# Layer 2 of a four-layer graph network on one core: diffusions moved into the end of the step before, blocks of layer 3 into the end of the second step

## The chip, the cores and the metric

The kernel runs on one core of one Trainium2 chip. Its engines are TensorE (PE in the profile, with PEld for its weight loads), VectorE (DVE), ScalarE (ACT), GpSimd (POOL) and SyncE (SP, which here only issues DMAs). The metric is the device time of one execution in microseconds. Each engine works through its own instructions in order, and waits in front of one whose data or buffer is not ready.

## What is computed

Four graph layers over 4096 nodes with 256 features, each followed by a residual and a layer norm. The change concerns layer 2 and the start of layer 3:

```python
def L2(X, S, W1, W2, W3, U1, U2, ln_g, ln_b):
    R = S + eye(N);  R = R / R.sum(-1, keepdims=True)
    Z = 0;  Xf = X;  Xa = X
    for n in range(2):
        A = top_p_attention(Xa, W1, W2, W3)
        Xf = R @ Xf
        Xa = A @ Xa
        Z = Z + Xf @ U1[n].T + Xa @ U2[n].T
    h = X + Z
    return layernorm(h) * ln_g + ln_b

def L3(x, adj, W, b):
    agg = adj @ x / maximum(adj.sum(1), 1)
    return relu(concat([x, agg]) @ W + b)

x = layernorm(x + L2(x, adj, ...))
x = layernorm(x + L3(x, adj, ...))
```

`top_p_attention` is a softmax over all nodes, of which each row keeps its largest entries up to a sum of 0.9, renormalised.

## The kernel before, in words

The 4096 rows are 32 blocks of 128 (`NB = 32`, b is a block). Layer 2 runs two steps. In both, the matrix that the adjacency multiplies lies in `XD`: for each block 512 columns, a rounded part and its remainder. A **diffusion** of block b is 32 matmuls of 512 columns into one PSUM bank, fed by eight pieces of the adjacency (256 KB each, four matmuls each, `adj_piece`, three buffers in turn, L176 and L179). Layer 3's product has the same shape; `early` (L1490 to L1498) is the same work for layer 3's first blocks, with the identity subtracted on POOL (L1493) from the piece that holds the block's own rows.

One **pass** of a step's loop handles block b in eight parts `s`: PE gathers the attention rows of block b (`gather`, L1300, from transposes `turn`, L1291), computes the scores of block b+2 (L935), and does the diffusion of block b+2, spread over the parts by the list `pieces`. DVE meanwhile selects the top entries of block b+1 (`nucleus`, L1072 to L1144: a threshold, two passes over the row, the largest 40, the edges, and eight multiplications in place at L1143). ACT exponentiates, copies transposes out of PSUM and estimates the next threshold (`guessed`). POOL adds up rows and, in step 1, normalises. Step 1's passes also close block b-1 (`closing`, the norms of layer 2) and, two blocks back, multiply the result by layer 3's weights (`turned`, `weighted`, `ahead3`, L1384, L1393, L1466 to L1468).

The order of the instructions in the loops is written by hand for PE, ACT, DVE and POOL (`manual_schedule`). Elsewhere, and for SP everywhere, a planner with a cost model orders them; it may also put later instructions into gaps of a hand-ordered stretch.

Around the steps stand:

- **Step 0's end.** The last pass (b = 30) has no diffusion and no scores left. DVE finishes block 31 and computes a verdict over all blocks (`settled`, L1187 to L1212), for which PE transposes twice (L1204, L1208). The verdict goes to DRAM, every engine reads it and branches past a repair (`mend`, L1157). Then block 31 is gathered, interleaved with step 1's `keys` (L848 to L899).
- **Between the steps.** The step's result rows are reloaded into `XD`, 1 MB for four blocks (`reload`, L1151).
- **Step 1's beginning.** Scores and threshold of block 0, `spreads` (L908 to L926), then sixteen projections of two blocks (`project`: PE at L1419, ACT copies at L1432 and L1434, a DMA in at L1431, an addition on POOL at L1435, a DMA out issued by ACT at L1436). The scores of block 1 stand in the middle of the projections. Then the diffusions of blocks 0 and 1, and the loop.
- **Step 1's end.** In the last pass blocks 0 and 1 of layer 3 are begun (seven pieces each). Then block 31 is gathered and closed, the repair is branched past, and behind it stand block 2 of layer 3 and, from weights in `kT` that DVE casts (`cast3`, L1703), block 3. All of them wait for the last row of `XD`, written from block 31's result (L1468). Layer 3 then does one block after another (L1738), with its weights cast by DVE and ACT (L1703, L1705) and its closing on DVE and ACT.

Of the kernel before, what the change touches and what calls it, by code (L numbers as in the profile page):

```python
# [9 lines left out]
F32 = mybir.dt.float32  # L10
# [45 lines left out]
class Net:  # L56
# [686 lines left out]
    def layer2(self):  # L743
# [3 lines left out]
        with ExitStack() as ctx:  # L747
# [312 lines left out]
            def nucleus(step, b, c, low, far, thr, pm=None, gw=None, sq=None):  # L1060
# [80 lines left out]
                for j in range(T):  # L1141
                    ec = e[:, j * 512:(j + 1) * 512]
                    nc.vector.scalar_tensor_tensor(ec, ec, edge[:, j:j + 1], ec, op0=ALU.is_ge, op1=ALU.mult)  # L1143
                nc.vector.reciprocal(r, r)  # L1144
# [8 lines left out]
            def mend(step, row, flag, e, r, h=None, pairs=None):  # L1153
# [3 lines left out]
                with tc.If(flag == 0):  # L1157
# [16 lines left out]
                    if step == 1:  # L1174
                        reload(xtd, 0, NB - 4)
                        for k in range(2):
                            nc.tensor.matmul(pairs[:, k], kT[:, :P], XD[:, 0].rearrange("p s d -> p (s d)"),
                                             start=False, stop=True)
                        whole(both(pairs))

            def settled():
# [24 lines left out]
                nc.vector.tensor_reduce(each, pt[:NB, :P], AX.X, ALU.min)  # L1206
                pt = psum.tile([P, 512], F32, name="ps_tp")
# [192 lines left out]
            def project(step, b):  # L1400
# [29 lines left out]
                else:  # L1430
                    nc.sync.dma_start(xb, rows(xd[two, :, 0, :]))  # L1431
                    nc.scalar.copy(X[:, two, :], pl[:, :, :D])  # L1432
                    xs = work.tile([P, 2, D], F32, name="part", bufs=1)
                    nc.scalar.copy(xs, pl[:, :, D:])  # L1434
                    nc.gpsimd.tensor_add(xb, xb, xs)  # L1435
                    nc.scalar.dma_start(rows(xd[two, :, 0, :]), xb)  # L1436
# [47 lines left out]
            def early(ps, b, groups):  # L1484

                for g in groups:
                    a = work.tile([P, 4, P], F32R, name="adj_piece", bufs=3)
                    nc.sync.dma_start(a.bitcast(F32), self.adjs[b, :, 4 * g:4 * g + 4, :])  # L1490
                    k = b - 4 * g
                    if 0 <= k < 4:
                        nc.gpsimd.tensor_sub(a[:, k, :], a[:, k, :].bitcast(F32), self.ident)  # L1493
                    for k in range(4):
                        jc = 4 * g + k
                        if jc == NB - 1:
                            yield a
                        nc.tensor.matmul(ps, a[:, k, :], XD[:, jc].rearrange("p s d -> p (s d)"),  # L1498
                                         start=(jc == 4), stop=(jc == NB - 1))
                    yield  # L1500

            def both(pairs):

                for b in range(2):
                    yield from early(pairs[:, b], b, (1, 2, 3, 4, 5, 6, 0))

            weights(0)
            for step in range(2):
# [7 lines left out]
                rs, edge = {}, nucleus(step, 0, *guess)  # L1516

                for b in range(0, NB, 2):
                    if b == 16:
                        whole(scores(1, queries(1)))  # L1520
                        guess = drained(guessed(step, 1))
# [11 lines left out]
                xb = base(step, 0)  # L1533
                pr = whole(diffusion(step, 0))
                whole(diffused(step, 0, pr, xb))
                whole(keep(step, 0, xb))
                pr = whole(diffusion(step, 1))
                aTs = [turn(es[0], g) for g in range(2)]
                q, xb = queries(2), base(step, 1)
                xc, pa, done, guessing = None, None, {}, iter(())  # L1540
                pieces = (0, 0, 2, 1, 2, 1, 2, 0) if step == 0 else (0, 0, 2, 1, 1, 2, 1, 1)
                with tc.manual_schedule(engines={ET.PE, ET.Activation, ET.DVE, ET.Pool}):
                    for b in range(NB - 1):
                        ahead = b + 2 < NB
                        edge = nucleus(step, b + 1, *guess)
                        if ahead:
                            score = scores(b + 2, q)
                            beside = diffusion(step, b + 2)
                        close, kept, put = None, None, None
                        if step == 1 and not ahead:  # L1550
                            pairs = psum.tile([P, 2, 512], F32, name="ps_logit", bufs=2)
                            beside = both(pairs)
                            nas = [t[:, i * 2048:(i + 1) * 2048].bitcast(U8).rearrange("p (k i) -> p k i", k=8)
                                   for t in (es[2], es[0]) for i in range(2)]
                            self.load_bytes(nas[:2], 0, 0)
                            pieces = (0, 2, 2, 2, 2, 2, 2, 2)
                        for s in range(8):
                            if s == 0:
# [6 lines left out]
                                difs = diffused(step, b + 1, pr, xb)  # L1565
                                next(difs)
                                kept = keep(step, b + 1, xb)
# [13 lines left out]
                            if ahead or step == 1:  # L1581
                                for _ in range(pieces[s]):
                                    next(beside)
# [8 lines left out]
                            if s in (2, 4, 6):  # L1592
# [5 lines left out]
                            if s == 6:  # L1598
                                if ahead:
                                    xb = base(step, b + 2)  # L1600
# [12 lines left out]
                            if s == 0:  # L1613
# [8 lines left out]
                        if not ahead:  # L1622
                            row = result(row)
                            if step == 1:
# [194 lines left out]
```

## Time and profile before

Three runs took 4100.99, 4105.11 and 4111.95 us, the median is 4105.11. The profiled execution took 4103.01 us; its span, from the first to the last instruction, is 4101.3. All times below are microseconds from the start of the span.

| engine | busy us | share of the span | instructions |
|---|---|---|---|
| PE | 3911.0 | 95% | 25081 |
| PEld | 3380.8 | 82% | 25081 |
| DVE | 3002.8 | 73% | 6655 |
| ACT | 2757.6 | 67% | 5127 |
| POOL | 1062.5 | 26% | 1300 |

| group | count | busy us | mean ns |
|---|---|---|---|
| gather, L1300 | 4096 | 971.9 | 380 |
| diffusion, L179 | 2048 | 579.2 | 418 |
| transposes, L1291 | 2048 | 308.2 | 273 |
| scores, L935 | 1024 | 275.3 | 410 |

Matmuls overlap in the array, so a group's time is less than count times mean: 32 products of layer 3 (L1738) end 7.47 us after each other. Step 0's loop runs from about 1812 to 2654, step 1's from about 2854 to 3767; layer 3's steady products begin at 3876.

### The profile page before, as it was taken

To read this page: it belongs to the slowest core of one execution; us is meant where nothing else is said; L and a number is where in the kernel's file an instruction comes from. 1 tells how busy PE (TensorE), PEld (TensorE's weight loads), DVE (VectorE), ACT (ScalarE), POOL (GpSimd) and SP (SyncE) were. 2 spreads that over 40 slices of the span, in tenths; PEclk is the share of its full clock that TensorE was granted. 3 is DMA by queue.
4 is the path that set the end of the run, shared out by engine and by line. 5 is a ranking of instruction groups with operands and counts; after the bars stand their busy time and mean duration, and the time that the engine had idled before them with its cause. 6 is when DMAs were issued, how large, how long until landed. Compare 5 with 4: busy or idle time off the path is not lost. (4 is left out here: it accounts for less than half of the span.)

```text
span 4101.3 us, 68724 instructions
## 1 busy us (share of the span) xinstructions
PE 3911.0 (95%) x25081; PEld 3380.8 (82%) x25081; DVE 3002.8 (73%) x6655; ACT 2757.6 (67%) x5127; POOL 1062.5 (26%) x1300
## 2 busy tenths in 40 slices
PE   7999989999999899899999999988999999998898
PEld 6999989999999687468888888854888888887686
DVE  7642229999999354647878878846899999998354
ACT  5543339999997322458888888734888888886232
POOL 0111110110333122301111111103465555554211
PEclk9999999999999999899999999989999999999999
DMA  4765554324220596333333233434333333335431
GB/s 121 230 212 177 177 189 167 94 85 145 87 87 29 221 387 267 110 109 99 98 96 103 92 99 98 163 110 135 106 103 108 112 103 113 106 106 202 154 133 43
DMA packets 291419, 551.45 MB, mean 134 GB/s; under 512 B 38678, under 2 KB 118678, under 8 KB 286966
## 3 DMA queue, kind: packets, MB, share of 16 engines
q1 hardware_dynamic: 205828, 390.15, 29.3%
q0 software_dynamic: 26384, 80.24, 5.9%
q10 hardware_dynamic: 58850, 76.47, 5.4%
q8 instruction: 203, 3.33, 0.3%
q14 instruction: 154, 1.26, 0.1%
HBM read 380.80 MB, written 165.94 MB: 133 GB/s over the span
## 5 line engine op out<-in xcount | busy, mean ns | idle before, releaser
L1300 PE MATMUL ps_a<-X,aT 128*128 128x256 f32 x4096 | 971.9, 380 | 2.6 <-ACT h L1441 1.1
L1300 PEld LDWEIGHTS ps_a<-X,aT 128*128 128x128 f32 x4096 | 774.3, 190 | 127.6 <-issue 2.4
L300 PE MATMUL acc<-gm,gt 128*128 128x198 bf16 x8192 | 704.1, 248 | 27.0 <-issue 15.4
L300 PEld LDWEIGHTS <-gt 128*128 128x128 fp8e4 x8192 | 700.2, 97 | 30.8 <-issue 15.6
L292 ACT ACTIVATE sg<-lpb,nlc 128x1024 fp8e4<-128x1024 f32 x640 | 671.3, 1135 | 60.3 <-DVE gt L294 34.8
L179 PE MATMUL ps_r<-XD,adj_piece 128*128 128x512 f32 x2048 | 579.2, 418 | 10.9 <-ACT dif L1338 5.6
L517 PE MATMUL pz<-src,ar 128*128 128x264 f32 x4096 | 509.0, 287 | 9.6 <-DVE ar L507 7.1
L517 PEld LDWEIGHTS pz<-src,ar 128*128 128x128 f32 x4096 | 505.8, 189 | 12.7 <-DVE ar L507 11.5
L1028 ACT ACTIVATE ja<-e,nc 128x2048 uint8<-128x2048 f32 x240 | 480.9, 2004 | 2.0
L1293 ACT COPY aT<-ps_tp 128x512 f32<-128x512 f32 x512 | 296.3, 579 | 230.9 <-PE ps_tp L1291 226.4
L179 PEld LDWEIGHTS ps_r<-XD,adj_piece 128*128 128x128 f32 x2048 | 365.3, 191 | 91.5 <-issue 14.3
L510 ACT ACTIVATE nb<-a 128x512 uint8<-128x512 f32 x256 | 156.5, 630 | 292.2 <-DMA a<-in_adjt_dram 279.3
L1093 DVE MAX8 cand<-v 128x8 f32<-128x256 f32 x1024 | 347.2, 412 | 4.4
L1143 DVE SCALAR_TENSOR_TENSOR e<-e,edge 128x512 f32<-128x512 f32 x512 | 346.0, 748 | 2.2
L1291 PE MATMUL ps_tp<-ident,e 128*128 128x128 f32 x2048 | 308.2, 273 | 7.4 <-DVE e L850 6.6
L1291 PEld LDWEIGHTS ps_tp<-ident,e 128*128 128x128 f32 x2048 | 256.7, 142 | 60.0 <-issue 8.0
L1089 DVE SCALAR_TENSOR_TENSOR v<-e,hi 128x2048 f32<-128x2048 f32 x128 | 302.5, 2363 | 2.4
L285 DVE TENSOR_SCALAR sg<-lpb,nlc 128x1024 fp8e4<-128x1024 f32 x384 | 283.1, 774 | 2.0
L935 PE MATMUL ps_logit<-kT,q 128*128 128x512 f32 x1024 | 275.3, 410 | 8.7 <-DVE kT L893 3.7
L937 ACT ACTIVATE e<-ps_logit 128x1024 f32<-128x1024 f32 x256 | 260.2, 1027 | 30.5 <-PE ps_logit L935 30.5
L507 DVE CAST ar<-a 128x1024 fp32r<-128x1024 f32 x128 | 88.8, 694 | 230.5 <-PE pz L517 230.4
L731 PE MATMUL ps_adj<-XD,adj_piece 128*128 128x512 f32 x1024 | 236.1, 391 | 0.0
(370 smaller groups left out, 5440.3 us busy)
## 6 DMA issues: line engine op xcount, KB each, us to landing
adj_piece<-adjs SPq DMA_DIRECT2D x536, 256.0 KB
a<-in_adjt_dram SPq DMA_DIRECT2D x256, 256.0 KB
adjs<-adj_piece SPq DMA_DIRECT2D x96, 512.0 KB
na<-nad SPq DMA_DIRECT2D x64, 512.0 KB
nad<-nb POOLq DMA_DIRECT2D x128, 128.0 KB, 3.4
lpb<-lpd POOLq DMA_DIRECT2D x32, 512.0 KB, 4.1
na<-nad ACTq DMA_DIRECT2D x16, 1024.0 KB
gmd<-gb ACTq DMA_DIRECT2D x64, 198.0 KB
```

What stands on the lines that cost most here:

```text
L179: nc.tensor.matmul(ps, a[:, k, :], rhs(jc).rearrange("p s d -> p (s d)"), start=(jc == 0), stop=(jc == self.NB - 1))
L285: nc.vector.tensor_scalar(sg[:, k, :], lpb, nlc[:, jc, h:h + 1], 2.0 ** -5, op0=ALU.is_ge, op1=ALU.mult, saturate=False)
L292: nc.scalar.activation(sg[:, k, :], lpb, AF.Sign, scale=-1.0, bias=nlc[:, jc, h:h + 1], saturate=False)
L300: nc.tensor.matmul(acc[:, q, :6 * C1], gt[:, k, q * P:(q + 1) * P], gm[:, jc, hh, :], start=(jc == 0 and q % 2 == 0), stop=(jc == NB - 1 a ...
L517: nc.tensor.matmul(pz[q][:, t, :W], ar[:, q, k, :], src[:, jc, t, s], start=(jc == 0 and s == 0), stop=(jc == NB - 1 and s == 1))
L1028: nc.scalar.activation(ja, e[:, s * HALF:(s + 1) * HALF], f, bias=nc1, accum_out=fs[:, i + s:i + s + 1])
L1089: nc.vector.scalar_tensor_tensor(v, ec, hi, ec, op0=ALU.is_lt, op1=ALU.mult, accum_out=sb[:, s:s + 1])
L1093: nc.vector.max(cand[:, 8 * j:8 * j + 8], v[:, k * 256:(k + 1) * 256])
L1143: nc.vector.scalar_tensor_tensor(ec, ec, edge[:, j:j + 1], ec, op0=ALU.is_ge, op1=ALU.mult)
L1291: nc.tensor.transpose(pt[:, k * P:(k + 1) * P], e[:, jc * P:(jc + 1) * P], self.ident)
L1293: nc.scalar.copy(aT, pt)
L1300: nc.tensor.matmul(pa[:, :D], aT[:, k * P:(k + 1) * P], X[:, jc, :], start=(jc == 0), stop=(jc == NB - 1))
```

## The change

The change moves work between the stages named above.

1. **Step 1 is three diffusions ahead instead of two** (`dd = 2 + step`). Its first three diffusions are done at step 0's end by the rewritten `early`: 21 pieces (`pieces` and three more) in and behind the last pass, and the last three pieces once rows 28 to 31 have been reloaded. They use the two banks of `pairs` and the bank `third`. Their sums are added to `xd` there (`base`, `diffused`, `keep`).
2. **The last pass's order.** `nucleus` yields after the second and fourth of its eight edge multiplications in the last pass, and `settled` yields once more, so that the verdict's steps stand among the edges.
3. **Rows are reloaded by groups** of four blocks as the last diffusion's pieces pass; rows 24 to 27 of step 1 in the last pass, rows 28 on behind it.
4. **Step 1's beginning** computes scores and threshold of block 1 ahead of the projections. A projection's copy alternates between the buffers `part` and `dif`, and its DMA out is issued by POOL.
5. **Layer 3's first five blocks** go through `early` in step 1's last two passes and behind the repair, a sixth from `kT`; the casts into `kT` are ACT's. The last row's six matmuls stand together at the end. Layer 3 starts with `ready(6)`.
6. **SP is ordered by hand** too, in the loops and in two new stretches: the end of step 1 before the repair, and behind it.

```diff
-                    xs = work.tile([P, 2, D], F32, name="part", bufs=1)
+                    xs = work.tile([P, 2, D], F32, name=("part", "dif")[b // 2 % 2], bufs=1)
                     nc.scalar.copy(xs, pl[:, :, D:])
                     nc.gpsimd.tensor_add(xb, xb, xs)
-                    nc.scalar.dma_start(rows(xd[two, :, 0, :]), xb)
+                    nc.gpsimd.dma_start(rows(xd[two, :, 0, :]), xb)
...
+            def piece(step, b, g, a=None):
+                if a is None:
                     a = work.tile([P, 4, P], F32R, name="adj_piece", bufs=3)
+                nc.sync.dma_start(a.bitcast(F32), self.adjs[b, :, 4 * g:4 * g + 4, :])
+                if step == 1 and b // 4 == g:
+                    nc.gpsimd.tensor_sub(a[:, b % 4, :], a[:, b % 4, :].bitcast(F32), self.ident)
+                return a
+
+            def times(ps, a, g, first=False, ks=range(4)):
+                for k in ks:
+                    jc = 4 * g + k
+                    nc.tensor.matmul(ps, a[:, k, :], XD[:, jc].rearrange("p s d -> p (s d)"),
+                                     start=(first and k == 0), stop=(jc == NB - 1))
+
+            def early(step, todo, banks, made):
+                a = piece(step, *todo[0])
+                started = set()
+                for i, (b, g) in enumerate(todo):
+                    after = piece(step, *todo[i + 1]) if i + 1 < len(todo) else None
+                    times(banks[b], a, g, b not in started)
...
+                    a = after
                     yield
...
                 rs, edge = {}, nucleus(step, 0, *guess)
+                if step == 1:
+                    whole(scores(1, queries(1)))
+                    guess = drained(guessed(step, 1))
...
+                dd = 2 + step
+                if step == 0:
+                    todo = [(k, g) for g in range(7) for k in range(3)]
+                else:
+                    todo = [(k, g) for g in (1, 2, 3, 4, 5, 0, 6) for k in range(2)]
+                    todo += [(2, g) for g in (1, 0, 2, 3, 4, 5, 6)]
+                    todo += [(3, 0), (4, 1), (3, 1), (4, 0), (3, 2), (4, 2), (3, 3), (4, 3), (3, 4), (4, 4),
+                             (3, 5), (4, 5), (3, 6), (4, 6)]
+                five = {ET.PE, ET.Activation, ET.DVE, ET.Pool, ET.SP}
+                with tc.manual_schedule(engines=five):
...
+                        if b + dd < NB:
+                            beside = diffusion(step, b + dd)
+                        elif b + dd == NB:
+                            beside = early(step, todo, banks, made)
+                        if step == 0 and not ahead:
+                            pieces = (0, 2, 2, 3, 3, 3, 2, 2)
+                        elif step == 1 and b == NB - 3:
+                            pieces = (0, 0, 1, 1, 1, 2, 1, 1)
+                        elif step == 1 and not ahead:
+                            pieces = (1, 2, 2, 2, 2, 2, 1, 1)
...
+                            for _ in range(pieces[s]):
+                                next(beside)
+                                if b + dd == NB - 1 and count > 2:
+                                    reload(rows_of, 4 * count - 12, 4 * count - 8)
+                                count += 1
...
+                    next(row)
+                    next(edge)
+                    next(beside)
+                    row = result(row)
+                    rs[b] = whole(edge)
+                    for _ in range(3 if step == 0 else 5):
+                        next(beside)
+                    if step == 0:
+                        reload(rows_of, NB - 4, NB)
+                        sums = [base(1, 0), base(1, 1)]
+                        for k in range(3):
+                            times(banks[k], piece(0, k, 7), 7)
+                            if k == 2:
+                                sums.append(base(1, 2))
+                            whole(diffused(1, k, banks[k], sums[k]))
+                            whole(keep(1, k, sums[k]))
...
+                with tc.manual_schedule(engines=five):
+                    self.load_bytes(nas, 0, 0)
+                    xb = bases(b)
+                    close = closing(b - 1, pa, rs.pop(b - 1), xc)
...
+                flag = nc.values_load(row[:, NB:], min_val=0, max_val=1)
+                mend(step, row, flag, None, None, *hand, made[:])
...
+                    self.cast3(nas, 5, a, nc.scalar)
+                    for _ in range(4):
+                        next(beside)
                     reload(xtd, NB - 4, NB - 1)
+                    next(close)
+                    whole(beside)
...
+                    product(0)
+                    for k in range(5):
+                        t = piece(1, k, 7)
+                        times(banks[k], t, 7, ks=range(3))
+                    lasts.append(t[:, 3])
+                    h = whole(close)
+                    product(1)
+                    xT = turned(h[:, 0], bank())
+                    product(2)
+                    pz = weighted(xT, bank())
+                    product(3)
+                    whole(ahead3(b, h, pz, True))
+                    for t, to in zip(lasts + [a[3][:, 7]], [banks[k] for k in range(5)] + [ps]):
+                        nc.tensor.matmul(to, t, XD[:, b].rearrange("p s d -> p (s d)"), start=False, stop=True)
```

`product(i)` is eight matmuls of block 5 from the quarter i of `kT` (seven for the last).

## Prediction

> **What bounds the kernel now.** I read the busy row by slices first, then the busy time by stage for the places where it dips, then TensorE's timeline inside those, then the waits and the DMA rates there.
>
> ```profile
> PE   7999989999999899899999999988999999998898
> ...
> PEclk9999999999999999899999999989999999999999
> ...
> 2000.00:2080.00 80.00, 80.00 (x404) 68.13 (x404) 66.88 (x187) 69.33 (x152) 10.71 (x12) 1.00 0.30 93
> 2960.00:3040.00 80.00, 80.00 (x397) 66.86 (x396) 76.68 (x187) 70.37 (x168) 43.75 (x53) 1.00 0.36 113
> ...
> 2654.00:2743.90 89.90, 69.73 (x388) 52.29 (x386) 41.88 (x111) 26.92 (x44) 3.55 (x4) 0.89 0.52 158
> 2743.90:2854.40 110.50, 96.03 (x308) 53.09 (x308) 85.34 (x171) 46.34 (x129) 37.30 (x24) 0.95 0.37 119
> 3766.84:3875.79 108.95, 83.56 (x338) 62.13 (x339) 35.98 (x107) 13.90 (x30) 29.15 (x40) 0.88 0.51 175
> ```
>
> After the window come busy PE, PEld, DVE, ACT, POOL, then granted clock, DMA share, GB/s. In both loops of layer 2 (first two window rows) PE is busy for all 80 us: every matmul counts there, and nothing else does. The last three are stages I cut myself: **A**, from step 0's last loop pass to the end of step 1's keys; **B**, from there to where step 1's loop begins (2854.4: its second pass starts at 2882.46, and a pass without the two small products lasts 28.1); **C**, from the last pass of step 1 to layer 3's steady products. PE idles 20.2, 14.5 and 25.4 us in them, 60.1 together.
>
> ```profile
> 2679.25 0.37 PE L1204 MATMUL ps_tp<-ident,okay 128*32 128x128 f32 x1 [6.23 <-DVE okay L1201]
> 2684.71 0.21 PE L1208 MATMUL ps_tp<-ident,each 32*1 32x32 f32 x1 [5.09 <-DVE each L1206]
> 2691.54 1.94 PE L1291 MATMUL ps_tp<-ident,e 128*128 128x128 f32 x8 [6.63 <-DVE e L850]
> 2693.36 3.78 PE L1300 MATMUL ps_a<-X,aT 128*128 128x256 f32 x8
> ...
> 3777.53 3.75 PE L1498 MATMUL ps_logit<-XD,adj_piece 128*128 128x512 f32 x8 [8.26 <-DMA adj_piece<-adjs]
> ...
> 3865.16 1.65 PE L1498 MATMUL ps_r<-XD,adj_piece 128*128 128x512 f32 x3 [3.40 <-DMA adj_piece<-adjs]
> ```
>
> The bracket is PE's idle time and what ended it. A idles on one chain: DVE's last edges, the verdict row, the flag, the branch. In C it is adjacency pieces queued behind 7 MB of rows. Behind gaps PE also runs slowly: eight gathers take 1.73 us in the loop, but 3.58 at 2693.36. Summing such groups against their loop rate: A 2.8 us, B 1.7 (twelve matmuls in 4.5 instead of 2.8 at 2843.59), C 9.3 (64 products 17.57 instead of 14.93 at 3875.79, the rest in five groups), 13.8 together. The PE work is the same after the change, so **the ceiling is 60.1 + 13.8 = 73.9 us**.
>
> **The change part by part.** A piece is four matmuls; 32 of layer 3's take 7.47 us, so a piece is 0.93 us, a block 7.5.
>
> *Part 1, three diffusions into A.* 21 pieces (19.6 us) go among and behind the gathers of step 0's last pass, then three last pieces (2.8 us) wait for rows 28 to 31. The DVE chain is what they hide behind. DVE's own time hardly moves: the reordered edges let the verdict's first reduction come before six of eight edge operations. The pass becomes eight times (1.73 + 0.43) = 17.3 us of gathers and turns plus 17 pieces (16) = 33 us, later than DVE's verdict (24 us into the pass now), so the 6.23 and 5.09 us waits go. What is late next: (a) SP's order is now the program's, so the first piece stands behind 7 MB of rows.
>
> ```profile
> 2650.00:2660.00 10.00, 8.95 (x47) 7.60 (x47) 5.44 (x10) 4.99 (x12) 2.25 (x1) 1.00 1.05 394
> ```
>
> At 390 GB/s, 8.5 MB from 2636 on land by 2661, and PE wants it at 2658.5: 2.5 us. (b) Rows 28 to 31 (1 MB, some 2.7 us plus 2 of latency) are issued behind the verdict's row on SP, then the three pieces; PE has three pieces in between: 3.8 us idle. (c) The branch now stands alone:
>
> ```profile
> L1157 PEldq COMPARE_BRANCH  x2: 3673/3680/3688, 2687.3 to 3835.1; - x2
> ```
>
> 3.68 us on PE's queue, of which its run-ahead hides about 1.2 (in C the branch began 2.1 us before PE's last matmul ended): 2.5. The flag itself will have landed. The new base loads, adds and stores for blocks 0 to 2 go to POOL, idle there until 2758; of ACT each block takes 0.7 us, and the mul of block k+1 waits for POOL's two adds (0.75 us each) since `dif` is single. That would reach gather(31) only through the store of block 30, queued on ACT: 0 to 3 us; I take 0, as this store floats ahead of the flag today (2673). With 1.1 for h and 2.6 of small waits, A keeps 12.5 of 20.2 (bounds 6 and 20).
>
> *Part 2, B without diffusions.* 64 matmuls (15 us) leave, a third block's 32 are replaced in pass 0 by block 3's. Here what went must not have been cover: between 2743.9 and 2755 fifteen of these matmuls fill the wait for the key table; projections can take their place, so 0 to 5 us idle, I take 3. Projecting loses 8.0 us today to `part`. This is where a rule speaks against the change: the Trainium skill (DMA: Bandwidth & Descriptors, "Issuing engines are not separate DMA queues") says moving a transfer to another issuing engine saves only its issue time, "usually small". By the rule: 16 times 0.38 us of ACT, on no path, so 0. By the row:
>
> ```profile
> ACT X L1432 <- POOL xb L1435: 18.8, 7, 5.7
> ...
> xd<-part POOLq DMA_DIRECT2D x6, 256.0 KB, 2.5
> ```
>
> ACT's copies stand behind an issue that waits for POOL's add; with the issue on POOL and two buffers in turn, most of the 8.0 us can go. I follow the row. The price is the `xb` cycle: load 2.3 + add 1.3 to 5 (mean 2.1) + issue 0.7 + POOL store 2.5, 7.6 us for two buffers, 3.8 per projection against PE's 3.5 to 3.7: nearly the bound, so 3 us stay (0 to 12). Scores and first sums of block 1 move ahead of the projections; DVE has an idle 5.0 us there, and block 0's nucleus was done at 2810, before PE is at 2830. B keeps 6 (bounds 2 and 20).
>
> *Part 3, loop.* 29 passes exchange block b+2 for b+3, pass 29 does 7 pieces of layer 3: 0. SP by hand keeps piece, query, piece; each needs what it needs now: 0.
>
> *Part 4, C.* Rows 0 to 23 are asked for in passes 28 on, before the pieces of layer 3, where passes 28 and 29 have slack (no piece before pass 29's third part): the 8.26 us go. Then nothing holds POOL and DVE back: DVE's 11.6 us idle at 3779 is PE's stall, returned. Pass 30 is 13.8 (gather) + 2.6 + 2.0 + 13 pieces (12.4) + 1.1 = 32, later than DVE's 31 (12.3 to the end of the second max pass, 1.5 of waiting, 17.2 of tops, verdict and edges as from 3790.8 to 3808.0). Six pieces, 7.2 us as three buffers in turn follow each other at about 1.3 us (a load lasts some 3 us with its latency, the waits of 0.4 to 1.3 us between such pieces at 1781 and 3804). Gather 31 with two small products 20.5. Then the branch (2) and the tail: nine pieces (8.4), five pieces of three matmuls (3.5), 31 matmuls of block 5 (7.2), two small products, the last six (1.4). The chain it covers, now from 3837.24 to 3872.6, held POOL for 14.6 us at a subtraction waiting for a piece; the change makes all subtractions earlier, so it shrinks to about 14 us and PE's 19 us of filler outlast it. What is left over: 1.1 h, 0.5 row, 1.5 + 4 piece latency and 768 KB of rows, 2 branch, 2 until layer 3's first cast (1.97 today; the pool still waits for the same last store): 11 of 25.4 (bounds 6 and 22). C's end is two blocks further on.
>
> *The clock.* The trace's row is 3840.44: after only 3.24 us idle, sixteen matmuls took 5.35 us instead of 3.74. The skill (TensorE: Matmul & The Clock Gate, Part 1) has the clock halved after an idle window of about 3.4 us. By the rule my gaps of 2 to 3.8 us would mostly be free; by the row each costs 1.6. I keep three, 5 of 13.8.
>
> **Sum.** 20.2 − 12.5 = 7.7, 14.5 − 6 = 8.5, 25.4 − 11 = 14.4, clock 8.8: 39.4 us. The profiled execution took 4103.0 (span 4101.3); less 39.4 is 4063.6. The median 4105.1 is 2.1 above it, so 4065.
>
> **Rivals.** *Loads as the next bound:* pieces end up behind rows in A and the tail, A and C keep 20 and 22 of their idle time, so gain 20.9: 4084. For: 8.5 and 4.3 MB bursts run at full DMA share; against: the rest of A needs 5.3 MB in 33 us. *Projection bound by `xb`:* adds stretched by DVE to 5 us and POOL's issues behind them, B gains nothing: 4074. For: adds of 4.0 and 5.1 us under DVE's long passes; against: only five of 16. *All covered:* lower bounds, gain 14.2 + 12.5 + 19.4 + 12 = 58: 4047. *Slower:* SP's hand order makes one piece per pass late in the 60 loop passes, where PE has no slack. A query or reload waiting ahead of it would do that; at 1.2 us per pass it costs 72, 4138, and it decides from 39.4 / 60 = 0.66 us. Against: in the loops pieces wait only for their buffer, and the query is already issued between pieces. *It doesn't do what it says:* if hoisting fails in both ends PE merely swaps idle places, 4100.
>
> **Numbers.** Forecast case 0.50, loads 0.17, projection 0.10, all covered 0.13, slower 0.06, no effect 0.04. Range 4040 to 4087. Of a measurement here 0.3% (12 us) can be told: faster 0.90, same 0.04, slower 0.06.
>
> **What would show it.** The 6.23, 5.09 and 8.26 us gaps gone; layer 3 matmuls of five blocks ahead of the last XD write; step 1's loop beginning with no diffusion ahead; projections without ACT's wait for POOL's add. I am wrong if the loops show PE below 80 in 80, if a piece wait above 4 us stands in A or the tail, or if POOL's adds pace the projections.

## The result and the profile after

The changed kernel took 4083.0 us (median of 8 runs, 4077.06 to 4092.06) against 4103.17 us for the kernel before on the same chip (8 runs, 4099.9 to 4111.95). The ratio is 0.9951, 95% interval 0.9939 to 0.9964: 20 us less, between 15 and 25. The forecast was 4065, a gain of 39. The profiled execution took 4083.41 us, its span is 4081.7. One of proj_q's 13 runs below took 5709 us, a slow run, and its ratio leaves it out.

The busy time by slices and by stage, as it was read before. The first column is the window, then its length, then busy PE, PEld, DVE, ACT and POOL, granted clock, DMA share and GB/s.

```profile
PE   7999989999999799799999999999999999999899
...
PEclk9999999999999999899999999999999999999999
```

```profile
2657.70:2760.20 102.50, 93.59 (x484) 70.10 (x482) 41.82 (x111) 28.98 (x47) 11.33 (x16) 0.95 0.59 184
2760.20:2844.58 84.38, 77.61 (x237) 40.48 (x236) 65.61 (x119) 43.74 (x125) 39.26 (x29) 0.94 0.26 88
...
3765.00:3805.00 40.00, 33.02 (x142) 25.89 (x141) 27.41 (x85) 4.71 (x10) 17.84 (x22) 0.88 0.53 182
3805.00:3832.50 27.50, 27.05 (x120) 20.42 (x118) 1.37 (x4) 6.63 (x14) 5.19 (x7) 0.93 0.25 83
3832.50:3874.08 41.58, 27.71 (x94) 19.34 (x95) 2.97 (x9) 5.55 (x9) 6.27 (x9) 0.88 0.59 206
```

Length less busy PE is PE's idle time. A (first row) idles 8.9 us, and 3.4 more in the pass before it, 12.3; B (second row) idles 6.8. Both sums are near the forecast's 12.5 and 6. C (the last three rows) idles 7.0 + 0.5 + 13.9, and 2.8 in pass 28: 24.1 us, where 11 were forecast and 25.4 stood before. TensorE's timeline says where. First A: the verdict's two transposes (L1209, L1214) no longer wait.

```profile
2663.05 2.13 PE L1504 MATMUL ps_logit<-XD,adj_piece 128*128 128x512 f32 x8 [0.60 <-DMA adj_piece<-adjs]
...
2693.58 0.27 PE L1209 MATMUL ps_tp<-ident,okay 128*32 128x128 f32 x1
...
2694.71 0.18 PE L1214 MATMUL ps_tp<-ident,each 32*1 32x32 f32 x1
...
2698.81 1.43 PE L1504 MATMUL ps_logit<-XD,adj_piece 128*128 128x512 f32 x4 [2.79 <-DMA adj_piece<-adjs]
...
2704.01 0.66 PE L1297 MATMUL ps_tp<-ident,e 128*128 128x128 f32 x2 [2.07 <-DVEq L1159]
2705.56 2.04 PE L1504 MATMUL ps_logit<-XD,adj_piece 128*128 128x512 f32 x4 [0.88 <-DMA adj_piece<-adjs]
```

Then C and the first blocks of layer 3:

```profile
3725.92 1.20 PE L179 MATMUL ps_r<-XD,adj_piece 128*128 128x512 f32 x4 [2.30 <-DMA adj_piece<-adjs]
...
3773.78 1.65 PE L1504 MATMUL ps_logit<-XD,adj_piece 128*128 128x512 f32 x3 [3.07 <-POOL adj_piece L1497]
...
3803.15 0.79 PE L1504 MATMUL ps_logit<-XD,adj_piece 128*128 128x512 f32 x1 [2.05 <-POOL adj_piece L1497]
...
3832.54 3.04 PE L1504 MATMUL ps_logit<-XD,adj_piece 128*128 128x512 f32 x12 [0.45 <-PEq L1159]
3840.20 3.44 PE L1504 MATMUL ps_logit<-XD,adj_piece 128*128 128x512 f32 x8 [4.62 <-DMA adj_piece<-adjs]
...
3848.40 1.20 PE L1504 MATMUL ps_logit<-XD,adj_piece 128*128 128x512 f32 x4 [1.86 <-DMA adj_piece<-adjs]
3852.42 2.08 PE L1504 MATMUL ps_logit<-XD,adj_piece 128*128 128x512 f32 x4 [2.82 <-DMA adj_piece<-adjs]
...
3874.08 11.44 PE L1823 MATMUL ps_tp<-XD,adj_piece 128*128 128x512 f32 x48 [1.88 <-DVE adj_piece L1790]
3886.29 4.00 PE L1823 MATMUL ps_tp<-XD,adj_piece 128*128 128x512 f32 x16 [0.77 <-DVE adj_piece L1790]
3893.25 6.94 PE L1823 MATMUL ps_r<-XD,adj_piece 128*128 128x512 f32 x22 [2.96 <-DVE adj_piece L1790]
```

The figure in front of a row's engine is how long the group lasts; the bracket is the wait. The 8.26 us wait has gone, and in its place stand several: two for a subtraction on POOL inside the last pass, and a row of them for pieces behind the branch (the branch itself costs 0.45).

To compare whole kernels I cut every trace at the same six instructions: the first scores of step 0's pass 29, step 1's first scores, the first scores of its third pass, those of its pass 28, the end of gather 31, layer 3's first product; then the last store's issue, and the span's end. **Start** is from step 1's first scores to its third pass, **tail** from gather 31's end to layer 3's first product. The loop between the third pass and pass 28 is 792 us in all of them.

| kernel | A | start | 28 to gather 31 | tail | layer 3 | end | median us | ratio to before, interval |
|---|---|---|---|---|---|---|---|---|
| before | 122.9 | 161.7 | 134.3 | 38.6 | 216.1 | 9.4 | | |
| changed | 138.5 | 138.9 | 137.1 | 42.0 | 204.4 | 3.2 | 4083.0 | 0.9951 (0.9939, 0.9964) |
| proj | 140.7 | 153.0 | 133.0 | 40.3 | 204.6 | 9.5 | 4102.84 | 0.9991 (0.9983, 0.9999) |
| proj_q | 140.6 | 152.9 | 130.9 | 41.4 | 204.6 | 9.4 | 4104.69 | 0.9993 (0.9984, 1.0001) |
| proj_b | 138.6 | 143.2 | 136.4 | 41.1 | 204.6 | 3.2 | 4090.2 | 0.9963 (0.9949, 0.9976) |
| before_proj | 123.4 | 157.5 | 133.3 | 37.5 | 215.1 | 3.2 | 4096.73 | 0.9976 (0.9968, 0.9985) |
| rows_end | 147.4 | 138.4 | 140.1 | 40.0 | 204.5 | 3.3 | 4099.31 | 0.9985 (0.9977, 0.9993) |
| x_late | 140.0 | 137.9 | 137.1 | 38.4 | 204.3 | 3.2 | 4084.15 | 0.9947 (0.9934, 0.9960) |
| deep | 136.2 | 138.8 | 133.9 | 33.0 | 204.7 | 3.3 | 4074.66 | 0.9932 (0.9920, 0.9944) |
| neg | 139.6 | 142.5 | 125.0 | 40.4 | 204.7 | 3.2 | 4074.9 | 0.9927 (0.9914, 0.9940) |
| sub_dve | 141.4 | 138.1 | 127.7 | 36.9 | 204.7 | 3.2 | 4074.05 | 0.9922 (0.9908, 0.9935) |
| deep_neg | 139.5 | 141.0 | 125.4 | 35.4 | 204.9 | 3.2 | 4069.98 | 0.9908 (0.9893, 0.9923) |
| fill | 138.3 | 139.8 | 123.1 | 33.7 | 202.8 | 3.2 | 4066.12 | 0.9909 (0.9894, 0.9924) |
| last_first | 139.8 | 139.2 | 126.4 | 30.3 | 209.2 | 3.2 | 4071.95 | 0.9922 (0.9909, 0.9936) |

Work has moved between the stages, so lengths are not yet gains. Three diffusions moved into A (24 pieces, 22.4 us); two left the start (15.0); one left step 1's pass 29, where two more blocks of layer 3 came in (net +7.5 in the two columns before "layer 3", −14.9 in it). With that, the changed kernel gains 122.9 + 22.4 − 138.5 = 6.8 in A, 161.7 − 15.0 − 138.9 = 7.8 in the start, 172.9 + 7.5 − 179.1 = 1.3 in C, and loses 204.4 − (216.1 − 14.9) = 3.2 in layer 3, whose first blocks now wait for casts (0.77 and 2.96 us). That is 12.7. Another 6.2 us of the 19.6 in the traces come from the program's last microseconds, which no step of the prediction spoke of.

Each row is one trace, and the same code does not last equally long in all of them. A is 136.2 to 141.4 us in the eleven kernels that leave its code alone, the start 137.9 to 142.5 in nine, pass 28 to gather 31 130.9 to 137.1 in six, the tail 36.9 to 42.0 in seven; ahead of A the kernels with the change take 2624.5 to 2633.1 us. So a difference under about 5 us in one column is not shown by one trace, and the changed kernel's own trace is the longest of its kind in C: proj, proj_q and proj_b, with the same code there, take 173.3, 172.3 and 177.4 us from pass 28 to layer 3, where it takes 179.1. In these four C gains 1 to 8 us, and PE idles 21 to 24 us in it.

### The profile page after: what moved, and what is told of

Same layout as the page of the kernel before. It is cut to its first block, busy times and chain, and to the rows that moved or that the text cites. A ratio compares the mean times of both kernels' runs of the same rounds, so it can differ in the third digit from the quotient of the medians.

```text
span 4081.7 us, 68719 instructions
## 1 busy us (share of the span) xinstructions
PE 3911.8 (96%) x25081; PEld 3381.4 (83%) x25081; DVE 2996.7 (73%) x6647; ACT 2758.5 (68%) x5127; POOL 1078.4 (26%) x1318
## 5 line engine op out<-in xcount | busy, mean ns | idle before, releaser
L300 PE MATMUL acc<-gm,gt 128*128 128x198 bf16 x8192 | 704.2, 248 | 26.1 <-issue 14.9
L179 PE MATMUL ps_r<-XD,adj_piece 128*128 128x512 f32 x1952 | 548.5, 415 | 9.7 <-DMA adj_piece<-adjs 9.6
L517 PE MATMUL pz<-src,ar 128*128 128x264 f32 x4096 | 508.3, 287 | 11.9 <-DVE ar L507 9.8
L179 PEld LDWEIGHTS ps_r<-XD,adj_piece 128*128 128x128 f32 x1952 | 345.2, 189 | 85.4 <-DMA adj_piece<-adjs 13.9
```

Of the source, the lines that this page charges most:

```text
L179: nc.tensor.matmul(ps, a[:, k, :], rhs(jc).rearrange("p s d -> p (s d)"), start=(jc == 0), stop=(jc == self.NB - 1))
L300: nc.tensor.matmul(acc[:, q, :6 * C1], gt[:, k, q * P:(q + 1) * P], gm[:, jc, hh, :], start=(jc == 0 and q % 2 == 0), stop=(jc == NB - 1 a ...
L517: nc.tensor.matmul(pz[q][:, t, :W], ar[:, q, k, :], src[:, jc, t, s], start=(jc == 0 and s == 0), stop=(jc == NB - 1 and s == 1))
```

## Experiments

**The start: the queue of the projections.** Three kernels undo parts of that edit (proj both halves, proj_q and proj_b one each), and one adds it alone to the kernel before (before_proj).

```diff
-  xs = work.tile([P, 2, D], F32, name=("part", "dif")[b // 2 % 2], bufs=1)   # proj, proj_b
+  xs = work.tile([P, 2, D], F32, name="part", bufs=1)
-  nc.gpsimd.dma_start(rows(xd[two, :, 0, :]), xb)                            # proj, proj_q
+  nc.scalar.dma_start(rows(xd[two, :, 0, :]), xb)
```

> The projections of layer 2's second step as in the kernel before: stores of xd issued by ACT, one buffer for the low part; everything else changed. By Part 2 of the prediction (the queue matters): ACT again stands behind issues that wait for POOL's adds, the step's projections take 6 to 8 us longer, 4088 to 4091. By the rule that the issuing engine matters little: within 1 us of the changed kernel, 4082 to 4084. In between if POOL's adds pace the projections either way.

> Of the projections' two edits only the queue is undone: the stores of xd are issued by ACT again; the low part keeps its two buffers. With both undone the stretch from step 1's first scores to its third pass took 153.0 us in place of 138.9. Theory QUEUE (ACT stands in order behind an issue that waits for POOL's add, so all copies behind it wait): 149 to 153 us, total 4093 to 4100. Theory BUFFER (the second buffer of the low part is what lets ACT run ahead of POOL's add): 139 to 142, total 4082 to 4086. The Trainium skill's rule on issuing engines expects the latter too.

> The other half: one buffer for the low part, the stores stay on POOL. Theory QUEUE: ACT's next copy into the one buffer waits for POOL's add anyway, 2 to 5 us more than the changed kernel, 141 to 144 us in that stretch, total 4085 to 4089. Theory BUFFER: 149 to 153 us, total 4093 to 4100. If both halves cost the full 10 to 14 us, either wait alone is enough to tie ACT to POOL's add.

> The kernel before with the projections' two edits alone (stores of xd on POOL, two buffers for the low part); the diffusions of blocks 0 and 1 stay in the second step's start. With the edits undone in the changed kernel its start lost 14 us. Theory COVER (the diffusions that the change takes out of the start were what PE did while the projections stood behind ACT, so the edits are worth little while these stay, and 14 us once they go): the kernel before gains 0 to 5 us, 4099 to 4106. Theory SEPARATE (the edits are worth their 14 us wherever the diffusions are): 4090 to 4093, and most of the whole change's gain would be theirs.

With both undone nearly the whole gain is gone: 4102.84 us. In the start it costs 14.1 us, twice the 6 to 8 expected, and the queue alone costs 14.0. With the single buffer alone the start is 143.2 us, hardly above the 142.5 that neg needs with the changed kernel's start, so a cost of the buffer is not shown. ACT's waits in the start (us in total, times, longest), first of the changed kernel and then of proj:

```profile
ACT X L1438 <- PE ps_logit L1425: 14.7, 10, 3.0
ACT part L1440 <- POOL xb L1441: 11.1, 6, 4.8
ACT dif L1440 <- POOL xb L1441: 6.5, 6, 1.4
```

```profile
ACT X L1438 <- POOL xb L1441: 23.6, 9, 3.5
ACT c L944 <- POOL xb L1441: 6.7, 2, 5.0
...
ACT aT L1299 <- POOL xb L1441: 5.0, 1, 5.0
```

In the changed kernel ACT's next copy of the rows (`X`) waits for PE, as it should; only the later copy of the low part waits for POOL. With the store on ACT, everything on ACT waits for POOL's addition, also a threshold (`c`) and a transpose (`aT`) that have nothing to do with it. PE then shows it at the projections:

```profile
2806.73 5.23 PE L1425 MATMUL ps_logit<-wt,X 128*128 128x512 f32 x8 [2.70 <-ACT part L1440]
2813.86 3.70 PE L1425 MATMUL ps_logit<-wt,X 128*128 128x512 f32 x8 [1.89 <-ACT part L1440]
...
2863.12 1.20 PE L935 MATMUL ps_logit<-kT,q 128*128 128x512 f32 x4 [2.49 <-ACT part L1440]
2868.67 3.78 PE L1306 MATMUL ps_a<-X,aT 128*128 128x256 f32 x8 [4.35 <-ACT aT L1299]
```

The same edit in the kernel before is worth 4.2 us in that stretch by one trace each, far from the 14 that SEPARATE expected and inside what COVER did: there the 64 matmuls of the diffusions are PE's work while the projections wait. Without the edit, taking them out shortens the start by 8.7 us while 15.0 of work leave, a loss of 6.3. So the two edits belong together.

The totals moved by more than the start. proj lost 19.8 us by the medians, and 16 by the ratios to the kernel before; before_proj gained 10 (6 to 13 by its interval), not 4. The rest is in the column "end". There POOL's last long instruction, a drain, is almost three times as long in some kernels. Its row in before, then in the changed kernel (min/median/max in ns):

```profile
L1815 POOLq DRAIN  x3: 40/112/9692, 4090.8 to 4101.0; - x3
```

```profile
L1902 POOLq DRAIN  x3: 40/112/3485, 4077.4 to 4081.4; - x3
```

It is 9.69 us in before, proj and proj_q, where POOL issues 427 DMAs, and 3.48 in the eleven other traces, where it issues 443; nothing else in the last microseconds differs. 14.1 + 6.2 = 20.3 and 4.2 + 6.2 = 10.4: with it, both totals come out within their intervals. proj_q differs from the changed kernel, and proj from proj_b, in nothing but who issues these 16 stores, so the drain follows them. Why it does stays open.

**The rows by groups.** In rows_end the reload in the pass is removed and everything is asked for at its end.

```diff
-  if b + dd == NB - 1 and count > 2:
-      reload(rows_of, 4 * count - 12, 4 * count - 8)
...
-  reload(rows_of, NB - 12, NB - 8 + 4 * (step == 0))
+  reload(rows_of, 0, NB - 8 + 4 * (step == 0))
```

> The rows of the split input are reloaded at the end of the last diffusion's pass again, all at once (0 to 27 in the first step, 0 to 23 in the second), not four at a time behind the pieces that release them. By my Parts 1 and 4 the grouping is what lets the pieces of the last passes find their rows: 7 MB at 390 GB/s are 18 us, of which a pass behind has some 5 to 8 us of cover, so PE idles 8 to 12 us more in A and 3 to 8 in C: 4094 to 4103. Against it stand the waits that the grouping itself makes (3.5 us in pass 29 of the first step, 2.8 in pass 28 of the second), which go. If the rows were hidden anyway: 4077 to 4083.

It took 4099.31 us. In A, PE waits 11.32 us for the first early piece:

```profile
2674.68 3.41 PE L1504 MATMUL ps_logit<-XD,adj_piece 128*128 128x512 f32 x8 [11.32 <-DMA adj_piece<-adjs]
```

A grows by 8.9. In step 1, pass 28 is 5.3 us shorter without its waits, and a wait of 7.1 us stands in pass 29 instead; C as a whole is 1.0 longer, so the 3 to 8 us expected there are not shown. By the stages the groups are worth 10 us, nearly all in A; by the medians 16, by the ratios 14. The two traces differ by 5.4 us ahead of A already, where their code is the same.

**C: the loads behind the branch.** In x_late, layer 3's second set of weights (four views of `X`) goes behind the pieces. In the changed kernel SP issued them between the pieces, since the planner may float them into a hand-ordered stretch (the first and the last of four):

```profile
3834.60 0.33 SPq L1780 DMA_DIRECT2D X<-nad  x1
...
3859.24 0.42 SPq L1780 DMA_DIRECT2D X<-nad  x1
```

Shortened, with `weights_in_X` for the four views:

```diff
   lasts.append(t[:, 3])
+  self.load_bytes(weights_in_X, 1, 0)      # x_late; no longer in ready(8)
...
+  deep = work.tile([P, 4, 4, P], F32R, name="v", bufs=1)                     # deep, besides
+  for i in range(4): given[27 + i] = piece(1, *todo[27 + i], deep[:, i])
+  for i in (31, 32): given[i] = piece(1, *todo[i])
```

> Only the place of four transfers changes: layer 3's second set of weights (X<-nad, 4 of 1 MB) is issued behind the last adjacency piece of the tail instead of among the pieces. Theory LOADS (the tail behind gather 31 is slow because 4 MB that nobody needs yet go ahead of the pieces): PE's waits for pieces there (3.44, 4.62, 1.86, 2.82 us in the changed kernel) shrink to about 1 us each, the stretch from gather 31's end to layer 3's first product goes from 41.6 us to 32 to 35, the time from 4083 to 4074 to 4077. Theory LATENCY (three piece buffers in turn and some 3 us for a load set the pace whatever else is on the queues): the waits stay, at most 2 us gained, 4081 to 4083. Theory GIVEN BACK: the tail shortens, but block 8's casts then wait for the late weights and layer 3 takes the gain back, 4080 or more.

> As x_late, and behind the branch four more piece buffers (in the place of a scratch tile), so that six pieces are asked for at once in place of two. Theory LOADS: no better than x_late by more than 1 us. Theory LATENCY: the waits that x_late leaves go, the stretch from gather 31's end to layer 3's first product falls to 28 to 31 us, 4070 to 4073. If PE's first wait behind the branch (3.44 us) stays in both, it is the load's own latency, since no piece is asked for before the branch.

The 3.44 us that both expectations name as a wait is no wait: it is how long the eight matmuls behind the 4.62 us wait last. x_late's tail is 3.6 us shorter than the changed kernel's, but inside the 36.9 to 42.0 of that tail's code, and the total did not move (4084.15). PE still waits 2.11, 3.01 and 1.36 us for pieces, so LOADS as I stated it is wrong. And layer 3's first cast now waits longer, for the last store of h to free its buffer:

```profile
3876.66 1.90 DVE L1792 TENSOR_SCALAR adj_piece<-e 128x1024 fp32r<-128x1024 fp8e4 x3 [6.47 <-DMA xo<-h]
```

That store was issued at 3869.76, 9 to 10 us behind the late weights, and took 6.9 us, against 3.4 in the changed kernel. With deep's seven buffers in place of three, the tail falls to 33.0 us, the total to 4074.66, and the piece waits are small but for the first, which the branch on SP ends:

```profile
3831.48 2.04 PE L1504 MATMUL ps_logit<-XD,adj_piece 128*128 128x512 f32 x4 [2.60 <-SPq L1159]
3834.34 5.78 PE L1504 MATMUL ps_logit<-XD,v 128*128 128x512 f32 x16 [0.81 <-DMA v<-adjs]
...
3844.19 1.20 PE L1504 MATMUL ps_logit<-XD,adj_piece 128*128 128x512 f32 x4 [0.98 <-DMA adj_piece<-adjs]
```

The tail is 9.0 us shorter than the changed kernel's, and 30.3 to 35.4 us in all four kernels with these buffers, below all others. How much of it is the place of the weights (3.6 by these traces) and how much the buffers (5.4) is not settled, since no kernel has the buffers alone. LATENCY's 28 to 31 us were 2 too short.

**C: the subtractions.** In neg five matmuls of a negative identity replace them; in sub_dve they move to DVE (shortened):

```diff
-  nc.gpsimd.tensor_sub(a[:, b % 4, :], a[:, b % 4, :].bitcast(F32), self.ident)
+  nc.vector.tensor_sub(a[:, b % 4, :], a[:, b % 4, :].bitcast(F32), self.ident)       # sub_dve
+  nc.tensor.matmul(banks[b], nident, XD[:, b], start=False, stop=False)               # neg
```

> The subtraction of the identity from five adjacency tiles leaves POOL; each is replaced by one matmul of a negative identity into the same sum (5 x 0.23 = 1.2 us of PE), with the negative identity kept in a free query buffer. Theory POOL (subtractions stand in POOL's queue behind a closing, and are stretched by DVE): the waits 3.07 and 2.05 us for POOL in pass 30 of step 1 go, and the slow groups behind them, 3 to 6 us less, 4077 to 4080. Rival: the same pieces then wait for their load, or DVE's edges set the end of pass 30, under 1 us gained, 4082 to 4083.

> The changed kernel with the five subtractions on DVE in place of POOL, else unchanged. The negative-identity matmul cut the stretch from pass 28's first scores to gather 31's end from 137 to 125 us, more than the 5.1 us that PE waited for POOL's subtractions. Theory POOL (POOL's slow two-input operation and the closing behind it are the cost): DVE does it in some 0.3 us, 125 to 129 us, 4074 to 4077. Theory ANY QUEUE (an operation that waits for a load blocks whatever engine it stands on in order; DVE's edges decide when pass 30 ends): 132 us or more, 4080 to 4086.

neg gains more than I expected, 4074.9 us; sub_dve, 4074.05, what theory POOL then said. By the ratios that is 10 and 12 us less than the changed kernel. From the first scores of pass 29 to gather 31's end the six traces with the subtractions on POOL and grouped rows (changed, proj, proj_q, proj_b, x_late, deep) take 98.5 to 101.7 us, and neg, sub_dve and the three that build on neg 89.9 to 92.6. PE's busy time shows why it is some 10 and not 5, in windows of the changed kernel and then in the same windows of neg, up to the end of gather 31:

```profile
3727.00:3765.00 38.00, 37.88 (x181) 31.09 (x180) 31.56 (x81) 28.29 (x67) 18.38 (x21) 0.96 0.54 183
3765.00:3805.00 40.00, 33.02 (x142) 25.89 (x141) 27.41 (x85) 4.71 (x10) 17.84 (x22) 0.88 0.53 182
3805.00:3832.10 27.10, 27.05 (x120) 20.42 (x118) 1.37 (x4) 6.26 (x13) 5.19 (x7) 0.93 0.25 84
```

```profile
3734.30:3772.30 38.00, 37.88 (x181) 31.15 (x180) 32.10 (x81) 28.49 (x68) 18.09 (x20) 0.96 0.56 186
3772.30:3812.30 40.00, 39.93 (x188) 31.55 (x187) 27.50 (x86) 6.51 (x14) 20.79 (x21) 1.00 0.64 219
3812.30:3828.10 15.80, 15.76 (x79) 12.63 (x77) 1.36 (x4) 4.45 (x10) 2.04 (x3) 1.00 0.17 61
```

7 us of idle time go, and about 4 of matmuls at a lower clock (0.88 and 0.93 become 1.00). POOL's instructions show the two waits: it takes one subtraction in order behind a closing, and is slow at the other.

```profile
3770.57 2.75 POOL L1462 TENSOR_TENSOR h<-h,xb 128x256 f32<-128x256 f32 x1
3773.28 0.45 POOL L1497 TENSOR_TENSOR adj_piece<-adj_piece,ident 128x128 fp32r<-128x128 f32 x1
...
3800.26 2.84 POOL L1497 TENSOR_TENSOR adj_piece<-adj_piece,ident 128x128 fp32r<-128x128 f32 x1 [10.03 <-DMA adj_piece<-adjs]
```

The first waits 2.75 us behind block 29's addition, though it takes 0.45. The second stands behind nothing once its piece is there, but lasts 2.84 while DVE works on the edges; in the seven traces with this order on POOL it lasts 2.1 to 4.3, and most of the others 0.45 to 0.47. On DVE (sub_dve) a subtraction takes 0.28 to 0.37, PE waits 1.26 us at most for one, and the stretch is 127.7 us, so ANY QUEUE fell: the engine matters.

**Both, and a better version.** deep_neg has both edits; fill also moves matmuls whose operands are there ahead of late pieces; last_first lets SP issue the last store of h, and the weights behind it (shortened):

```diff
-  for _ in range(4): next(beside)
+  next(beside); product(0)                                       # fill
+  for _ in range(3): next(beside)
...
-  whole(ahead3(b, h, pz, True))
+  whole(ahead3(b, h, pz, True, nc.sync))                         # last_first
+  self.load_bytes(weights_in_X, 1, 0)
```

> The late weights and four more piece buffers of deep, and the negative-identity matmul of neg in place of POOL's subtractions. In the traces from the first scores of pass 28 to layer 3's first product, the changed kernel takes 179.1 us, deep 166.9, neg 165.4. If the two costs are separate (buffers and late weights behind the branch, POOL's queue ahead of it), they add: 153 to 156 us there and 4060 to 4065 in all. If one hides behind the other, 163 or more and 4071 to 4075.

> As deep_neg, and eight matmuls of block 5, whose operands need no load, go ahead of the first piece asked for behind the branch, and eight more ahead of the last five pieces. Theory LATENCY (what is left behind the branch is the load's own latency, since no piece can be asked for before the branch frees its buffer): the 1.64 and 1.66 us waits and the slow matmuls behind the first go, the stretch from gather 31's end to layer 3's first product falls from 35.4 to 31 to 32.5, 4066 to 4067.5. Rival: the casts of block 5 on ACT are late there and PE waits for them in place of the pieces, no gain, 4070 or more.

> As fill, but the last store of h (xo<-h, 128 KB) is issued by SP and ahead of layer 3's second set of weights (4 MB), in place of by ACT and behind them. In the traces the first casts of layer 3 stand waiting for exactly this store: it took 3.4 us from issue to landing in the changed kernel, 5.7 in fill and 6.9 in x_late, where the late weights move at the same time. Theory COLLISION (the late weights delay the store that opens layer 3, so that part of their gain is given back there): the store lands in 2 to 3 us, PE's wait at layer 3's first product goes from 4.22 to 1 to 1.8 us, 2.5 to 3 us less in all. Rival: the weights then come too late for block 8 and layer 3 (206.0 us in fill) grows by as much.

deep_neg's two gains add up only in part (160.8 us from pass 28 to layer 3, where 153 to 156 were expected by adding). Part of that sum was not theirs: 3.2 us of deep's gain stood ahead of gather 31 and 1.6 of neg's in the tail, where neither changes the code. Without them the sum is 158. Its total, 4069.98, lies between the two expectations. fill's total, 4066.12, is the one expected, but not for the reason given: its tail is 33.7, not 31 to 32.5. Behind the first wait, 2.62 at the branch, those for pieces fall to 0.87 and less, and the time turns up at the next door, layer 3's first product:

```profile
3851.31 16.71 PE L1840 MATMUL ps_tp<-XD,adj_piece 128*128 128x512 f32 x64 [4.22 <-DVE adj_piece L1807]
```

By ratio fill and deep_neg are not told apart (0.9909 and 0.9908), though fill has the lowest median, 4066.12. In last_first that wait falls to 2.04 and the tail to 30.3, the shortest of all, but its rival came true: layer 3 is 209.2 us long, 6.4 more than in fill. The closings' loads are now issued beside 4 MB of weights, and DVE waits 6.9 us for one:

```profile
ACT low L1848 <- DVE h L1852: 9.1, 2, 7.6
DVE x L1849 <- DMA x<-xo: 6.9, 1, 6.9
...
PE ps_tp L1840 <- ACT adj_piece L1809: 3.5, 1, 3.5
```

So none of the three places tried for the weights was free: among the pieces, at layer 3's door, or in its first blocks. fill, deep_neg, sub_dve and last_first beat the kernel before and the changed one; their intervals end below where that of the changed kernel begins.

## Why the prediction was right and wrong

The direction and the range held, the range by luck. The gain was half of what was forecast, and of that half a third (6.2 us, POOL's drain) came from nothing that I had named; without it the time would be near 4089, above the range's 4087. One sign named for being wrong did come, a piece wait above 4 us in the tail (4.62).

- **Part 1 (A) was right in its mechanism.** The pass takes 34 us for 33, and the 6.23 and 5.09 us waits are gone. That the sum came out, 12.3 us idle for 12.5, is partly luck, since two misses offset each other: the first early piece waits 0.60, not 2.5 (8.5 MB at 390 GB/s are 21.8 us, so they land at 2658, not 2661), and the rows cost 3.4 a pass earlier, in that pass's own pieces, where nothing was put down. Rows 28 to 31 cost 2.79 and 0.88, the branch 2.07 for 2.5. What the groups hide was shown by rows_end.
- **Part 2 (B) was right in its idle time** (6.8 for 6) **and too small in what the queue carries.** I gave the queue "most of the 8.0 us". Undone, it costs 14.0; that what covered the rest had left with the diffusions is what before_proj's 4.2 says. "What went must not have been cover" was asked of the key table's wait only, not of the projections. Of the two sides weighed there, the row was right; the rule of the Trainium skill (DMA: Bandwidth & Descriptors, "Issuing engines are not separate DMA queues") prices the issue alone, and here what stood in line was everything behind an issue that waits.
- **Part 3 was right:** 792 us for the same passes in every trace.
- **Part 4 (C) failed**, in the term for what is left over: 11 us, and 24.1 were left (at least 21 in the four traces with this code). The 24.1 are 11.9 for pieces behind the branch (4.62 + 0.24 + 0.30 + 1.86 + 2.82, and 1.33 + 0.77 for the last five), 1.9 for pieces in pass 30, 2.8 in pass 28, 5.1 for POOL, 0.5 for the branch, 1.9 for the first cast. The 5.5 for pieces and rows was sized from three buffers that follow each other at 1.3 us in a loop; behind the branch few pieces are in flight, with rows and 4 MB of floated weights beside them. Pass 28 was held to have slack for the rows, and paid 2.8. The sentence "the change makes all subtractions earlier", from which I took that POOL no longer holds anything, was half true: block 31's closing was free of them, so the chain was no bound, as forecast; but one subtraction now stood behind the closing of block 29 and another beside DVE's edges, with PE waiting, 10 us in all by neg and sub_dve. (13 pieces at 0.93 are 12.1 there, not 12.4, which changes nothing.)
- **The clock.** I kept 5 of 13.8 us. The idle time saved in A, B and C (60.1 − 43.2 = 16.9) less layer 3's new waits (3.7) is 13.2, and the stages gained 12.7: by these traces nothing of the clock was saved. It followed the waits of Part 4: with the POOL waits gone, about 4 us of slow matmuls went with them.
- **The rivals.** *Loads as the next bound* gave 4084 and came nearest in number; it was right for C, wrong for A. Its cause was only in part the loads: late weights and more buffers are worth about 9 us together, POOL's subtractions 10. *Projection bound by `xb`*, *all covered*, *slower* by SP's order and *no effect* did not come.

## What to carry to other kernels

Before taking work out of a stretch, ask what waits it was covering: a queue edit worth some 4 us with that work in place was worth 14 without it. When work is hoisted to where one engine is free, follow every helper instruction that it brings, on the engine where it will stand in order, and count the loads that can be in flight when it starts; a steady loop's spacing does not price a start from nothing. And split a total by stage to its very end before crediting it to an idea, and see how much the same stage varies between kernels that share its code.

## What was not expected of the hardware

- POOL's drain at the program's end took 9.69 us in the three kernels where POOL issues 427 DMAs and 3.48 in the eleven where it issues 443: shorter with more of them.
- POOL's 128x128 subtraction took 0.45 us, and 2.1 to 4.3 beside DVE's edge operations.
- The branch that stood as a 3.68 us instruction on PE's queue cost PE 0.45 us in C, and 2.07 in A, in the changed kernel.
- Behind waits of about 2.6 us PE became slow at once in one kernel, later in another, and not at all in a third place. Four matmuls took 2.04 us behind 2.60 (deep). In fill four took 1.18 behind 2.62, and then the next eight 3.54, where the same eight take 2.00 at 3833.88:

```profile
3820.18 1.18 PE L1505 MATMUL ps_logit<-XD,adj_piece 128*128 128x512 f32 x4 [2.62 <-SPq L1159]
3821.20 3.54 PE L1752 MATMUL ps_a<-XD,kT 128*128 128x512 f32 x8
```

Behind 2.75 in deep's A, at 2655.60, four took 1.21 and the next eight gathers the usual 1.89. A free-running window, as the Trainium skill describes it (TensorE: Matmul & The Clock Gate, Part 1), would do that, but no run here moves a wait against such a window; its 3.4 us as the length of a harmful gap is too long here.
